# Two graph layers on one core: a second strip of A^T kept as bfloat16 for the last stage, its low bits checked during the sort

## The chip, the cores and the metric

The kernel runs on one core of one Trainium2 chip. The metric is the device time of one execution in microseconds (us). The engines are PE (matrix products; PEld is its weight load), DVE, ACT, POOL and SP; SP here only issues transfers, and POOL, ACT and SP each have transfer queues of their own. In the profile, q1 carries what SP issues here and q0 what POOL issues.

## The reference

Inputs: x (2708 x 128), a 0/1 matrix A (2708 x 2708), scalars alpha and beta, weights W (128 x 128) and a (1 x 256).

```python
# layer 0
adj_norm = dis[:, None] * adj * dis[None, :]          # dis = clip(degree, 1) ** -0.5
attn = softmax(beta * cosine(x) * adj, axis=1)
x = layernorm(x + adj_norm @ x - x + sigmoid(alpha) * (attn @ x - x))
# layer 1
XW = x @ W
s_col, s_row = XW @ a[0, :128], XW @ a[0, 128:]
den = exp(leaky_relu(s_row[:, None] + s_col[None, :]))
num = A @ den
att = where(num != 0, den / num, 0)
x = layernorm(x + A @ (att @ XW))
```

The matrix is 29 MB in float32. Nothing promises that its entries are 0 or 1: the kernel reads it as float32, and wherever it uses a bfloat16 form it proves while running that nothing was lost (below).

## The kernel before

Rows and columns are cut into 22 blocks of 128 (the last is partly filled) and into 6 strips of 512 columns (the last has 148, the "tail", from column 2560 on). The core holds only some of the matrix at a time, so it reads most of A^T (`adj_t`) several times. The stages, with their times in the profile:

1. Attention of layer 0, 0 to about 220 us.
2. Diffusion by strips of A^T, in the order 0, 5, 1, 2, 3, 4, to about 300 us. Strips 3, 4 and 5 stay in SBUF. While strips 0 and 5 are there, `low_bits_of` checks them (L175): ACT sums the absolute values of the lower 16 bits of each float32 word. If the sum is zero, the bfloat16 in the upper half is exactly the word.
3. The sort, about 295 to 357 us, overlapping the end of diffusion. Since leaky_relu has two slopes, rows are ordered by score and cut into 24 groups of at most 126. This stage computes scores, thresholds, one-hot tables and, from e^score, running row sums of A ("carries") into the PSUM tile `tot`. The sums need every column of A^T: strips 3 to 5 from SBUF (`kept_strips`, letter "k") and columns 0 to 1535 from HBM, row block by row block (`first_strips`, letter "e", L738). `fill("kke...")` strews these pieces between the other work. Each `first_strips` call lets SP load 128 x 1536 words (768 KB) into one of five rooms and PE do 12 small products `tot`. I count these loads in the order in which they are called and call them row 0 to row 21. Rooms: rows 0, 1, 2 and 7 share one room inside `x_sb`; the others take four rooms (`nat`) in turn, rows 3 to 6, then 8 to 11, 12 to 15, 16 to 19, and 20, 21 in the first two again. A load can start when all readers of the room's former row are done. Around these pieces the order of the stage is: the end of strip 2's layernorm and scores (`tr_sb`, `rstd`, `x`, `x_ps`, `sb_ps` into `sr_b`), the counting that gives the range of scores (`reach_b`), X@W in rows (`xw_ps`, copied by ACT into `att` and written to `xw_d`), thresholds (`thr_ps`, `k_gt`), one-hot tables (`k_hot`, `k_ons` and `j_ons` on ACT, `onp` on DVE, `tab_ps` on PE, copied by ACT into `k_t`, selected into `k_sel`), and last the carries copied out of `tot` and the table for the other index (`j_t`, `gb`), behind which the loop's first `num` waits.
4. The main loop over the 24 groups (357 to 585 us, about 8.83 us a step): an indirect gather on POOL fetches 126 rows of A^T into a ring of four, PE forms `num`, DVE and ACT divide, PE multiplies by gathered XW. In 11 of the steps POOL also issues a transfer that copies two blocks of strip 0 to HBM as bfloat16 (`a16_d`).
5. The last stage, 586 to 669 us: H = A @ M with M split into `m_hi` and `m_lo`. A^T streams in chunks through six rooms (the four of the ring, `wt`, `xws`); a chunk is rounded to the F32R type by DVE into one of three `rounded` tiles, its low bits are checked by ACT (the results of all checks select a general kernel at the end if anything was lost), and PE multiplies (`products`, L1612). `PARTS` are column ranges: 512 to 1536, 1536 to 2560 (22 float32 chunks of 1 MB, 2 blocks x 1024 columns each) and 0 to 512, read from `a16_d` (6 bfloat16 chunks, 4 blocks each, 0.5 MB) and widened by ACT or POOL. The tail's columns (`last`) come by one transfer on POOL's queue at the stage's start (L1552); their 44 products are written in the middle of the second part. `finished` (L1565) copies a part's sums, transposes them back and does residual, layernorm and output.

Order: in the attention's first strip and from the end of diffusion through the loop, "strict" mode pins every DVE, PE, POOL and ACT instruction issued through `dve`, `mm`, `gps`, `act` to the program's order on its engine. An engine in strict mode runs nothing out of turn: an instruction whose input is late holds all behind it. SP's loads are in order too. The last stage is not strict; there a scheduler interleaves.

Of the kernel before, what the change touches and what calls it, by code (L numbers as in the profile page):

```python
# [10 lines left out]
BF16 = mybir.dt.bfloat16  # L11
F32R = mybir.dt.float32r
I16 = mybir.dt.int16
AF = mybir.ActivationFunctionType
ALU = mybir.AluOpType
AX = mybir.AxisListType
# [2 lines left out]
P = 128  # L19
N = 2708  # L20
# [16 lines left out]
EARLY = 3  # L37
LAG = 2
TAIL = (NS - 1) * SW
PARTS = ((SW, 3 * SW), (3 * SW, TAIL), (0, SW))  # L40
RAISED = (1, 2, 3, 4)
KEPT = 3
LIMIT = 16.0
# [5 lines left out]
def grouped(  # L49
# [125 lines left out]
    def low_bits_of(a, room):  # L175

        low = a.bitcast(I16).rearrange("p (n t) -> p n t", t=2)[:, :, 0]
        i = len(seen)
        seen.append(i)
        nc.scalar.activation(  # L180
            room[:, : a.shape[1]], low, AF.Abs, accum_out=low_bits[:, i : i + 1]
        )

    cnt = const.tile([P, NS, 2, 2], F32, name="cnt")
# [498 lines left out]
    low = late.tile([P, NB], F32, name="low")  # L683
    e2_p = late.tile([P, NB], F32, name="e2_p")
    e2_w = late.tile([P, 3, NB, 2], BF16, name="e2_w")
    e2_r = late.tile([P, NB], F32, name="e2_r")
    ct = late.tile([P, 4], F32, name="ct")
    pinned("POOL", nc.gpsimd.memset, e2_w, 0.0)
# [46 lines left out]
    summed = [*range(12), 20, 21, *range(12, 20)]  # L735
    rooms = [0, 0, 0, 1, 2, 3, 4, 0] + [1, 2, 3, 4] * 4

    def first_strips(kb, eng):  # L738
        room = rooms[summed.index(kb)]
        if room == 0:  # L740
            a = x_sb.rearrange("p b d -> p (b d)")[:, : KEPT * SW]
        else:
            tag = (None, "x_hi0", "x_lo0", "x_hi1", "x_lo1")[room]
            a = nat.tile([P, KEPT * SW], F32, tag=tag, name="nat")
        eng.dma_start(a, adj_t[ts(kb, P), : KEPT * SW])
        for part in range(3):
            for q in range(4):
                sum_part(part, 0, q, kb, 0, a[:, ts(q, quarters[0])])
# [495 lines left out]
    valued("j", 1, j_hot, cs_p, 12)  # L1244
    fill("ee")
    assert not any(jobs.values()), jobs
    tmp.tile([P, P], F32, name="spare")
    j_own = chosen("j", j_hot, j_run, j_ahead)

# [202 lines left out]
    for step in range(NG + LAG):  # L1452
        g, before, first = step, step - 1, step - LAG
        if g < NG:
            qs[g] = flow.tile([P, N], F32, tag="q", name="q", bufs=LAG + 2)
        for s, item in enumerate(strips_m):
            if first == 0 and s < NS - 1:
                weigh(first, *item)
            if g < NG:
                multiply(g, *item)  # L1460
                if (g, s) == (0, 1):
                    j_no.append(numbers())
                    gather_xw(0)
                    gather(3)
                    gather_xw(1)
                if (g, s) == (0, 4):
                    weights(2, gb[:, 2, :])
                if item[2] == half or s == NS - 1:
                    carry(g, *parts_m[s // 3])
                    if g == 0:  # L1470
                        if s < 3:
                            weights(1, gb[:, 1, :])
                        log(0, *parts_m[s // 3])
            if 0 <= before < NG and s < 2:
                divide(before, *parts_m[s])
            if first > 0 and s < NS - 1:
                weigh(first, *item)
                if first == NG - 1:
                    to_mt(s)
                    if s > 1:  # L1480
                        m_rows(s - 2)
        if 0 <= before < NG:
            for i0, i1 in (parts_m[0], (half, TAIL), (TAIL, N)):
                power(before, i0, i1)
        if g < NG:
            if g > 0:
                for i0, i1 in parts_m:
                    log(g, i0, i1)
            if 3 <= g + 2 < NG:
                weights(g + 2, (gb[:, g + 2, :] if g < 2 else wt[:, g + 2, P - G :]))  # L1490
            if g + RING < NG:
                gather(g + RING)
            if g + 2 < NG:
                gather_xw(g + 2)
        if step == 1:
            spread_out_weights(8, NG)
        if 3 <= step < 3 + NB // 2:
            b0 = 2 * (step - 3)
            gps(
                "dma_start",  # L1500
                a16_d[:, b0 * SW : (b0 + 2) * SW].rearrange("p (b i) -> p b i", i=SW),
                adj_t[b0 * P : (b0 + 2) * P, :SW].rearrange("(b p) i -> p b i", p=P),
            )
        if step == NG:
            accs.append(ps_num.tile([P, SW], F32, tag="num", name="m_tail"))
            weigh_tails(range(first + 1))
# [98 lines left out]
    def banks_for(p0, p1):  # L1605
        hs = [(h, min(h + SW, p1 - p0)) for h in range(0, p1 - p0, SW)]
        return [ps_m.tile([P, SW], F32, tag="m", name="h_acc") for _ in hs], hs

    def products(kb, rows, hacc, hs):
        for part, m in enumerate((m_hi, m_lo)):  # L1610
            for acc, (h0, h1) in zip(hacc, hs):
                nc.tensor.matmul(  # L1612
                    acc[:, : h1 - h0], m[:, kb, :], rows[:, h0:h1],
                    start=(kb, part) == (0, 0), stop=(kb, part) == (NB - 1, 1),
                )

    short_by = [nc.scalar.copy, nc.gpsimd.tensor_copy, nc.scalar.copy] * 2
    short_by = short_by[::-1]
    for p0, p1 in PARTS:
        w_ = p1 - p0  # L1620
        hacc, hs = banks_for(p0, p1)
# [1 line left out]
        for kb in range(0, NB, step):  # L1623
            n = min(step, NB - kb)
            room = h_rooms[k % len(h_rooms)]
            k += 1
            if p0 == 0:
                a = room.bitcast(BF16)[:, : n * w_]
                nc.sync.dma_start(a, a16_d[:, kb * w_ : (kb + n) * w_])
                t = rounded(short_by.pop(), a)  # L1630
            else:
                a = room[:, : n * w_]
                nc.sync.dma_start(
                    a.rearrange("p (b i) -> p b i", b=n), rows_at(kb, n, p0, p1)
                )
                t = rounded(nc.vector.tensor_copy, a)
                low_bits_of(a, hp.tile([P, 2048], I16, tag="junk", name="junk", bufs=1))
            for b in range(n):
                products(kb + b, t[:, b * w_ : (b + 1) * w_], hacc, hs)
            if waiting and kb > 0:  # L1640
                waiting.pop(0)()
            if p0 == PARTS[1][0] and kb == NB // 2 + 1:
                last_banks = banks_for(TAIL, N)
                for b in range(NB):
                    products(b, last[:, b, :], *last_banks)
                waiting += finished(TAIL, NB - TAIL // P, *last_banks)
        if p0 == PARTS[-1][0]:
            while waiting:
                waiting.pop(0)()
# [5 lines left out]
            nc.tensor.matmul(no_ps[:, 0:1], ones, wild[:, 1:2], start=True, stop=True)  # L1655
            odd = late.tile([P, 1], mybir.dt.int32, name="odd")
            dve("tensor_scalar", odd, no_ps[:, 0:1], 0.5, None, ALU.is_gt)
        waiting += finished(p0, (w_ + P - 1) // P, hacc, hs)
    while waiting:
        waiting.pop(0)()  # L1660
    l1.close()
# [436 lines left out]
```

## Time and profile before

| | us |
|---|---|
| median of 3 runs | 672.46 (672.36 to 673.21) |
| profiled execution, whole | 670.93 |
| its span | 669.2 |
| PE busy in the span | 626.8 (94%) |
| DVE busy | 483.7 (72%) |
| ACT busy | 485.8 (73%) |
| POOL busy | 257.1 (38%) |
| bytes moved, mean rate | 179.90 MB, 269 GB/s |

The profile is of one execution. A "busy" share is an average over stages that have different limits, so stretches of the span are read one by one below. A row of a timeline is: start, duration, engine, line, operation, output <- inputs, sizes, count, and in brackets how long the engine stood idle before it and what it waited for. "SPq" and the like are the issue of a transfer, not its length.

### The profile page before, as it was taken

How to read it: one execution, taken by the hardware profiler on the slowest of the kernel's cores; microseconds unless marked ns; L12 is line 12 of the kernel's file. 1: busy time of each engine (PE TensorE's matmuls, PEld its weight loads, DVE VectorE, ACT ScalarE, POOL GpSimd, SP SyncE). 2: the span in 40 equal slices, each digit the busy share in tenths (PEclk: the TensorE clock that was granted, in tenths of full speed). 3: DMA queues.
4: the chain of work that ended last, by engine and by line, in shares of the span. 5: the costliest groups of instructions: out<-in, count | busy, mean ns of one | idle time of the engine just before them, and what ended most of it. 6: DMA issues, size and time to landing. Idle time of an engine off the chain costs nothing.

```text
span 669.2 us, 8587 instructions
## 1 busy us (share of the span) xinstructions
PE 626.8 (94%) x2859; PEld 355.1 (53%) x2859; DVE 483.7 (72%) x989; ACT 485.8 (73%) x671; POOL 257.1 (38%) x261
## 2 busy tenths in 40 slices
PE   7999999999999999999768899999999999996994
PEld 4445453545547477666544344444444444674873
DVE  5776876747655465848684999999999998497435
ACT  4767777868875653321474999999999999598761
POOL 5976788787985311100122233333322220010021
PEclk9999999999997999999987899999999999999798
DMA  8958989998999999989877998666655553399951
GB/s 269 349 195 277 361 309 338 352 329 297 311 287 389 331 387 384 386 266 355 320 293 187 240 232 230 189 191 183 183 185 205 169 189 106 112 308 387 414 204 51
DMA packets 68710, 179.90 MB, mean 269 GB/s; under 512 B 6986, under 2 KB 21716, under 8 KB 65636
## 3 DMA queue, kind: packets, MB, share of 16 engines
q1 hardware_dynamic: 45044, 114.45, 48.9%
q0 software_dynamic: 22224, 63.08, 32.3%
q10 hardware_dynamic: 1392, 1.77, 0.8%
q8 instruction: 24, 0.39, 0.2%
q14 instruction: 26, 0.21, 0.1%
HBM read 179.33 MB, written 5.72 MB: 277 GB/s over the span
## 4 chain that ended last, share of the span: by engine, by line
PE 60%; DMA 16%; issue 8%; DVE 7%; ACT 6%; POOL 2%; another core or an unknown queue 0%; DVEq 0%; SPq 0%; ACTq 0%; POOLq 0%
PE num L195 14%; PE m_acc L195 12%; PE att_acc L204 10%; PE sim L204 8%; DMA strip<-in_adj_t 6%; PE h_acc L1612 5%; DMA last<-in_adj_t 5%; DMA row<-in_adj 3%; PE dif_acc L204 3%; ACT row L195 1%; PE dif_acc L195 1%; PE tot L195 1%; PE sim L195 1%; POOL ss L195 1%; ACT xn L195 1%
## 5 line engine op out<-in xcount | busy, mean ns | idle before, releaser
L220 POOL TENSOR_TENSOR total<-total,p_t 128x512 f32<-128x512 f32 (+3 forms) x111 | 125.3, 1130 | 33.6 <-ACT p_t L214 27.9
L195 PE MATMUL m_acc<-q,xws 128*128 128x512 f32 x240 | 122.5, 596 | 0.0
L209 DVE SCALAR_TENSOR_TENSOR p_t<-sim,gentle,piece 128x512 f32<-128x512 f32 (+1 forms) x111 | 72.2, 671 | 47.3 <-PE sim L204 37.5
L195 PE MATMUL num<-ring,wt 128*128 128x512 f32 x216 | 98.4, 548 | 2.7 <-DVE q L195 2.0
L204 PE MATMUL att_acc<-p_t,x_sb 128*128 128x512 f32 (+1 forms) x228 | 96.5, 549 | 2.1 <-ACT p_t L214 1.9
L214 ACT ACTIVATE p_t<-p_t,shift 128x512 f32<-128x512 f32 (+1 forms) x111 | 69.4, 655 | 36.8 <-DVE p_t L209 31.7
L195 DVE COPY q<-num 128x512 f32<-128x512 f32 (+1 forms) x142 | 85.7, 615 | 13.6 <-PE num L195 13.6
L195 DVE SCALAR_TENSOR_TENSOR q<-sr_b,nc_s,q 128x1536 f32<-128x1536 f32 (+1 forms) x48 | 77.8, 1623 | 6.5 <-ACT q L195 6.0
L195 PEld LDWEIGHTS m_acc<-q,xws 128*128 128x128 f32 x240 | 45.5, 191 | 55.6 <-issue 55.3
L195 ACT ACTIVATE q<-q,head,rest 128x1536 f32<-128x1536 f32 (+1 forms) x48 | 70.2, 1508 | 2.8 <-DVE ring L195 2.5
L195 ACT ACT_TABLE_LOAD x52 | 66.7, 1283 | 3.6 <-issue 2.7
L195 PEld LDWEIGHTS num<-ring,wt 128*128 128x128 f32 x216 | 39.2, 191 | 48.0 <-issue 35.1
L204 PEld LDWEIGHTS att_acc<-p_t,x_sb 128*128 128x128 f32 x228 | 40.1, 197 | 44.7 <-ACT p_t L214 23.5
L195 ACT ACTIVATE q<-q,c_s 128x1536 f32<-128x1536 f32 (+1 forms) x48 | 63.0, 1355 | 0.3
L195 ACT ACTIVATE row<-row 128x1354 f32<-128x1354 f32 x44 | 58.1, 1321 | 4.4 <-DMA row<-in_adj 4.3
L195 POOL DMA_INDIRECT ring<-in_adj_t,k_no x18 | 21.0, 1169 | 89.3 <-PE num L195 88.4
L204 PE MATMUL sim<-xn_t 128*128 128x512 f32 (+1 forms) x102 | 47.4, 581 | 0.0
L1612 PE MATMUL h_acc<-rounded,m_hi 128*128 128x512 f32 x110 | 38.9, 418 | 2.0 <-DVE rounded L1557 1.8
L1612 PE MATMUL h_acc<-rounded,m_lo 128*128 128x512 f32 x110 | 37.4, 405 | 0.0
L195 PE MATMUL num<-x_sb,wt 128*128 128x512 f32 (+1 forms) x72 | 35.4, 585 | 0.7 <-ACT gb L195 0.7
L195 POOL DMA_INDIRECT xws<-xw_d,j_no x24 | 28.3, 1180 | 18.5 <-DVE c_s L195 11.5
L195 DVE COPY ring<-q 2x1536 f32<-2x1536 f32 (+1 forms) x36 | 30.8, 855 | 2.7 <-ACT q L195 1.4
(334 smaller groups left out, 1047.5 us busy)
## 6 DMA issues: line engine op xcount, KB each, us to landing
row<-in_adj SPq DMA_DIRECT2D x44, 677.0 KB, 5.6
piece<-in_adj_t SPq DMA_DIRECT2D x24, 1024.0 KB, 6.9
strip<-in_adj_t POOLq DMA_DIRECT2D x6, 2816.0 KB, 17.5
nat<-in_adj_t SPq DMA_DIRECT2D x18, 768.0 KB, 6.3
ring<-in_adj_t SPq DMA_DIRECT2D x12, 1024.0 KB, 9.2
strip<-in_adj_t SPq DMA_DIRECT2D x2, 2816.0 KB, 14.4
strip<-in_adj_t POOLq DMA_DIRECT2D x2, 2048.0 KB, 13.6
x_sb<-in_adj_t SPq DMA_DIRECT2D x4, 1024.0 KB, 7.3
```

Source lines behind the costliest of these rows:

```text
L195: latest[engine] = op(*args, **kwargs)
L204: op(*args, **kwargs)
L209: return getattr(nc.vector, op)(*args, **kwargs)
L214: return getattr(nc.scalar, op)(*args, **kwargs)
L220: getattr(nc.gpsimd, op)(*args, **kwargs)
L1612: nc.tensor.matmul(acc[:, : h1 - h0], m[:, kb, :], rows[:, h0:h1], start=(kb, part) == (0, 0), stop=(kb, part) == (NB - 1, 1),)
```

## The change

Columns 512 to 1023 ("strip 1") join columns 0 to 511 as bfloat16. In the loop the copying transfers go from 11 of two blocks to 12 of four (two of the twelve have two), still one a step, steps 3 to 14. In the last stage strip 1 is read from the copy: the float32 part is now 1024 to 2560 in a part of width 1024 and a part of width 512, and twelve bfloat16 chunks follow, widened by POOL and ACT in turn. The tail's products are written behind the float32 parts rather than in the middle of the second.

As strip 1 is no longer read as float32 there, its low bits are checked elsewhere: on the rows of the sort. Each `first_strips` call begins by having ACT check columns 512 to 1023 of the row loaded by the call before (`low_bits_of_row`, 22 in all, the last one after the last sum). `low_bits_of` now goes through `act`, so the checks hold their place in ACT's strict order.

```diff
-PARTS = ((SW, 3 * SW), (3 * SW, TAIL), (0, SW))
+SHORT = 2 * SW
+PARTS = ((SHORT, 4 * SW), (4 * SW, TAIL), (SW, SHORT), (0, SW))
@@ low_bits_of
-        nc.scalar.activation(
-            room[:, : a.shape[1]], low, AF.Abs, accum_out=low_bits[:, i : i + 1]
+        act(
+            "activation", room[:, : a.shape[1]], low, AF.Abs,
+            accum_out=low_bits[:, i : i + 1],
         )
@@ the sort
+    low_row = late.tile([P, SW], I16, name="low_row")
+    unseen = []
+    def low_bits_of_row():
+        low_bits_of(unseen.pop()[:, SW:SHORT], low_row)
     def first_strips(kb, eng):
+        if unseen:
+            low_bits_of_row()
         room = rooms[summed.index(kb)]
...
         eng.dma_start(a, adj_t[ts(kb, P), : KEPT * SW])
+        unseen.append(a)
...
     assert not any(jobs.values()), jobs
+    low_bits_of_row()
@@ the loop
-        if 3 <= step < 3 + NB // 2:
-            b0 = 2 * (step - 3)
+        if 3 <= step < 3 + 12:
+            s, b0 = divmod(4 * (step - 3), 24)
+            n = min(4, NB - b0)
             gps(
                 "dma_start",
-                a16_d[:, b0 * SW : (b0 + 2) * SW].rearrange("p (b i) -> p b i", i=SW),
-                adj_t[b0 * P : (b0 + 2) * P, :SW].rearrange("(b p) i -> p b i", p=P),
+                a16_d[:, s, b0 : b0 + n, :],
+                adj_t[b0 * P : (b0 + n) * P, ts(s, SW)].rearrange(
+                    "(b p) i -> p b i", p=P
+                ),
             )
@@ the last stage
-    short_by = [nc.scalar.copy, nc.gpsimd.tensor_copy, nc.scalar.copy] * 2
-    short_by = short_by[::-1]
+    short_by = [nc.scalar.copy, nc.gpsimd.tensor_copy] * 6
...
-            if p0 == 0:
+            if p0 < SHORT:
                 a = room.bitcast(BF16)[:, : n * w_]
-                nc.sync.dma_start(a, a16_d[:, kb * w_ : (kb + n) * w_])
+                nc.sync.dma_start(a, a16_d[:, p0 // SW, kb : kb + n, :])
...
-            if p0 == PARTS[1][0] and kb == NB // 2 + 1:
-                last_banks = banks_for(TAIL, N)
-                for b in range(NB):
-                    products(b, last[:, b, :], *last_banks)
-                waiting += finished(TAIL, NB - TAIL // P, *last_banks)
...
-        waiting += finished(p0, (w_ + P - 1) // P, hacc, hs)
+        waiting += finished(p0, w_ // P, hacc, hs)
+        if p0 == PARTS[1][0]:
+            last_banks = banks_for(TAIL, N)
+            for b in range(NB):
+                products(b, last[:, b, :], *last_banks)
+            waiting += finished(TAIL, NB - TAIL // P, *last_banks)
```

More of the change, by code (lines that the diff above doesn't have):

```diff
@@ L13 @@
 I16 = mybir.dt.int16
+U16 = mybir.dt.uint16
 AF = mybir.ActivationFunctionType
@@ L2086 @@
     ]
-    a16_d = nc.dram_tensor("a16_d", (P, NB * SW), BF16, kind="Internal").ap()
+    a16_d = nc.dram_tensor("a16_d", (P, 2, NB, SW), BF16, kind="Internal").ap()
     xw_d = nc.dram_tensor("xw_d", (NP, D), F32, kind="Internal").ap()
```

## The prediction

> **What bounds the kernel now.** I read the table of windows first, to see which stage is bound by what; then ACT's and SP's timelines through the sort, since the change adds work to ACT there and SP's loads hang on it; then the chain of waits, and PE's timeline and the transfers in the last stage.
>
> The sort, in windows of 10 us: columns are length, then busy us (count) of PE, PEld, DVE, ACT, POOL, then PE's clock, the DMA share and GB/s.
>
> ```profile
> 290.00:300.00 10.00, 9.55 (x47) 6.17 (x46) 3.60 (x10) 0.36 (x1) 0.00 (x0) 1.00 0.69 240
> 300.00:310.00 10.00, 8.12 (x168) 5.18 (x172) 7.27 (x31) 1.50 (x4) 0.00 (x0) 1.00 0.98 371
> 310.00:320.00 10.00, 10.00 (x168) 8.76 (x161) 9.27 (x53) 2.77 (x6) 0.00 (x0) 1.00 0.74 264
> ```
>
> ACT is nearly empty here (0.36, 1.50, 2.77 of 10). By share alone the new checks are free. But ACT is in strict order, and its timeline shows what the idle time waits for:
>
> ```profile
> 299.64 0.58 ACT L195 COPY tr_sb<-dif_acc 128x512 f32<-128x512 f32 x1 [10.88 <-PE dif_acc L195]
> 303.74 0.30 ACT L195 ACTIVATE rstd<-mv,eps 128x4 f32<-128x4 f32 x1 [3.01 <-DVE mv L195]
> ...
> 322.27 0.37 ACT L195 COPY att<-xw_ps 128x256 f32<-128x256 f32 x1 [0.32 <-PE xw_ps L195]
> ...
> 348.57 0.27 ACT L195 COPY k_t<-tab_ps 128x128 f32<-128x128 f32 x1 [1.69 <-remote]
> ```
>
> SP issues row 2's load as soon as row 1's sums are done (PE's `tot` of row 1: 295.97 to 296.57), and PE consumes it at 301.26 with no wait:
>
> ```profile
> 296.62 0.33 SPq L745 DMA_DIRECT2D x_sb<-in_adj_t  x1
> ```
>
> ```profile
> 301.26 0.69 PE L195 MATMUL tot<-x_sb,e_w 128*2 128x384 bf16 x12
> ```
>
> The chain of waits shows that one later load is already late in the stage; a row takes 4.1 to 9.4 us from issue to landing (median 6.3; in the `x_sb` room 4.1 to 7.0, median 5.5):
>
> ```profile
> 322.89 5.53 DMA nat<-in_adj_t
> ```
>
> The last stage: the transfers are full (1.03 to 1.18) from 590 to 640, and PE stands once, for the tail:
>
> ```profile
> 619.78 0.49 PE L1612 MATMUL h_acc<-last,m_hi 128*128 128x148 f32 x1 [5.70 <-DMA last<-in_adj_t]
> ```
>
> From there to the last product at 659.0 PE stands little more. Why `last` takes 33.73 us (586.01 to 619.74), though it has only 1.67 MB, the queues say (here from 594 to 600):
>
> ```profile
> q1 hardware_dynamic: 522, 2.01, 89.1%
> q0 software_dynamic: 524, 0.31, 24.6%
> ```
>
> As many packets of `last` (592 bytes) go as packets of SP's queue (4 KB): one for one. So `last` gets 592/(592+4096) = 13% of the bytes.
>
> **The last stage.** Float32 chunks go from 22 MB to 16.5, bfloat16 from 2.88 MB to 5.77: 2.6 to 2.9 MB less, at the measured 385 to 417 GB/s 7 us of transfer. PE's work is the same (220 products of 512 columns, 44 of 148), so what counts is when PE waits. Chunks of the second float32 part now have rows of 2 KB, not 4. That is chunk 11 on; before, it was rounded at 610.13, one pace of 3.05 us after it began, about 607. Until then `last` goes as before, 50 GB/s x 21 us = 1.05 MB; then its share is 592/(592+2048) = 22%, 87 GB/s (estimate from those packets), and the other 0.62 MB take 7.1 us: it lands at 614.1, not 619.74. In both kernels PE has the first tail products behind chunk 11 (its order on the engine says so), which before ended at 613.8.
> Onward: chunk 12 lands at 614, then one every 2.55 us (the pace before, without `last`), each rounded in 1.22 and multiplied in 1.88. Chunk 15 and the half chunk 16 end at 625.9, the other 23 tail products (0.11 each) at 628.4, 88 products of bfloat16 parts (0.235 each, from 2.81 us for 12) at 649.1, the transposes (1.5) at 650.6. Take 651 against 659.0: 8.0 gained. In it are the 5.7 of standing and the 2.6 that the following products took too long: the clock is 0.70 in 620 to 630, and eight products took 3.5 us, not 1.88. Casts: 12, alternating ACT (1.89 to 1.92) and POOL (1.91), one chunk per 1.88 of PE, so two engines hide them. The five fewer DVE roundings and ACT checks of 128x2048 here are hidden either way. Bounds: 1.2 if `last` lands as before (only the stands of 0.25 and 0.79 at 643 and 646 go), 9.3 at most (stands and cold stretch all gone).
>
> A page speaks against this gain. The Trainium skill's "DMA: Bandwidth & Descriptors" (SWDGE vs HWDGE vs iDMA) says an engine switches between queues at packet boundaries, with packets of preferably up to 4096 bytes and many descriptors. By it, halving a row leaves the shares as they are and the gain at 1.2, which would make the sum 687.0. The one-for-one row above decides for me.
>
> **The loop.** The copying transfers move 0.52 MB more read and 0.26 more written per step. The trace shows a share of 0.60 to 0.73 in 440 to 510, and POOL issues such a copy in 0.75 us, then stands 5.65 us for PE's `num` before the next gather. A gather has three steps (26 us) of lead. I cost it at nothing; cover gone, one issue per step: 12 x 0.75 = 9 us.
>
> **The sort.** A check of 128x512: the 2048-wide one has a pitch of 2.03 us with its accumulator read (597.51, 599.54), a 1536-wide one runs 1.48 against 1.91, so 0.83 ns per column: 2.03 - 1536 x 0.00083 = 0.75 us. 22 of them are 16.5 us of ACT, which idles more than that. What costs is their place. A row's room is free only after ACT's check, which has ACT's in-order waits ahead of it. Three places, in times of before:
>
> 1. Row 0's check stands behind `rstd` of 288.47, so row 1's load goes at 289.6 instead of 257.9 and lands around 295; its sums are due at 295.97: nothing. Row 1's check stands behind the next `rstd` (303.74 + 0.30), so row 2's load goes at 304.8, not 296.62, and lands 4.1 to 5.5 later, 308.9 to 310.3. PE, in order, stands from 301.3. Then 2.5 us of sums that stood ahead of `x_ps` (301.26 to 303.8), `x_ps` 1.0, DVE's copy 0.68, so `sb_ps` at 313.0 at the earliest against 306.89. After standing that long PE is slow: 42 table products took 2.56 us after 3.75 idle, 1.40 when warm. That adds up to 3. Delay 5.6 to 8.5; I take 7.5, nearer to the cold row.
> 2. Row 12's load waits for row 8's check, behind the last `att` copy (322.64), and row 13's for the next check: issued at 323.4 and 324.15, landing about 328.9 and 330.7. Sums of row 13 began at 328.45, thresholds at 329.13; they come 2.2 later (1.5 to 4).
> 3. Rows 18 to 20 wait for checks behind the table work; row 21's load waits for row 17's check behind the `k_t` copy of 348.57: 349.6 against 344.04, beside the loop's first three gathers (4.1 MB). At 6.3 it lands at 355.8, sums were due at 349.7. The carries' copies, in order behind it, wait: 6.0 (3 to 9).
>
> Together 15.7 (10 to 21.5). Rows 3 to 11 have slack: those loads were issued 5 to 10 us ahead of use. The loop cannot win it back, for the last carry stands ahead of its first `num` at 356.92.
>
> **Sum.** +15.7 - 8.0 + 0 = +7.7. The profiled execution took 670.93 (span 669.2), 1.53 under the median; it would become 678.6, the median 672.46 + 7.7 = **680.2 us**.
>
> **The rivals.**
> - Faster: the checks are hidden. If ACT's and SP's order leaves row loads their lead, only the gain stays: 672.46 - 8.0 = 664.5. For it: ACT's idle share. Against: row 2's load, 4.7 us ahead of use, against a check that cannot run before 304.04. It decides when row 2 lands before 301.3.
> - `last` lands no sooner (packets do not go one for one at 2 KB): gain 1.2, so 672.46 + 14.5 = 687.0. For it: PE's order still puts tail products behind chunk 11. Against: the packet counts.
> - Only the first place costs (later rows have enough lead): 7.5 - 8.0 = -0.5, 672.0. For it: the medians of landing hide a best case of 4.1. Against: 322.89 5.53, a late load already on the chain.
> - The loop's copies are on the path: +9, 689. For it: PE, DVE and ACT are all full there. Against: POOL's 5.65 of idle and the gather's lead.
>
> **How the numbers follow.** Main case 0.58, its own range 676 to 685 (bounds of the three places, not all at one end); checks hidden 0.10; `last` no sooner 0.14; first place only 0.07; loop 0.11. A measurement can tell about 0.2%, 1.3 us, from no change. Faster: 0.10 and 0.02 of the middle case, 0.12. Same: 0.03. Slower: 0.85. The range 674 to 688 leaves out the 0.10, most of the 0.07 and half of the loop case: 0.2.
>
> **What would show it.** In the changed profile: row 2's load at about 305 and a stand of PE of some 8 us for DMA `x_sb` before 310; a clock under 1.00 there; the loop's first `num` at 372 rather than 356.92, and 228 us for the loop as before; `last` landing in some 28 us rather than 33.73; last products 8 us sooner after the loop's end than the 73 of before. I am wrong if row 2's load goes early, if the loop's steps grow beyond 8.83, or if PE still stands over 4 us for `last`.

## The result, and the profile after

The changed kernel takes **692.02 us** (median of 4 runs, 690.61 to 693.43) against 672.84 us for the kernel before, measured beside it (672.36 to 677.64). The ratio is 1.027, with a 95% interval from 1.0215 to 1.0322. It is slower, as forecast, but by 19.2 us and not by 7.7, and above the range of 674 to 688.

The profiled execution has a span of 689.0 us (before: 669.2). I cut both spans at the same three events: the first transposition `tr_ps` in the strict order of the sort (284.87 before, 285.43 after), the loop's first `num`, and the issue of the transfer of `last`.

| us | to the sort's first `tr_ps` | the sort, to the first `num` | the loop, to the issue of `last` | last stage |
|---|---|---|---|---|
| before | 284.87 | 72.05 | 229.09 | 83.19 |
| after | 285.43 | 100.14 | 226.03 | 77.40 |
| difference | +0.56 | **+28.09** | -3.06 | -5.79 |

The stage table of each experiment below is cut in the same way. The first column moves between executions by several us (284.9 to 295.6), and of the edits of this study only two work there (the checks left to the scheduler, and the check in the diffusion); so whole times are compared as medians, and stages by these cuts.

The sort is where the time went, in three stands of PE. The views follow in the order in which I read them. First the windows of after (columns: length, then busy us and count of PE, PEld, DVE, ACT, POOL, then PE's clock, the DMA share and GB/s):

```profile
290.00:300.00 10.00, 9.93 (x48) 6.52 (x48) 4.16 (x12) 0.00 (x0) 0.00 (x0) 1.00 0.69 238
300.00:310.00 10.00, 1.81 (x31) 1.02 (x34) 4.72 (x25) 2.49 (x6) 0.00 (x0) 0.67 0.69 236
310.00:320.00 10.00, 9.72 (x191) 6.03 (x183) 4.20 (x16) 4.32 (x13) 0.00 (x0) 0.82 0.72 244
360.00:370.00 10.00, 2.44 (x26) 1.14 (x26) 2.74 (x2) 5.28 (x19) 2.48 (x2) 0.57 1.03 275
370.00:380.00 10.00, 1.87 (x32) 1.26 (x35) 0.77 (x4) 1.56 (x6) 0.00 (x0) 0.50 0.91 219
```

PE is busy 1.81 us in 300 to 310, where it was busy 8.12 before, and its granted clock falls to 0.67 there; from 360 to 380 it does 4.3 us of work in 20 at a clock of 0.50 to 0.57. ACT is busy at most 5.28 us of 10 in these windows. It is nearly full only from 350 to 360 (9.27, with the one-hot tables; before, 8.35 in 330 to 340). So most of the loss is not ACT's time; what the loads wait for is the checks' place in its order.

PE's timeline of after says what it stood for (in brackets):

```profile
309.46 1.13 PE L198 MATMUL tot<-x_sb,e_w 128*2 128x384 bf16 x12 [7.46 <-DMA x_sb<-in_adj_t]
...
337.39 1.03 PE L198 MATMUL tot<-nat,e_w 128*2 128x384 bf16 x12 [3.92 <-DMA nat<-in_adj_t]
...
378.13 1.13 PE L198 MATMUL tot<-nat,e_w 128*2 128x384 bf16 x12 [10.68 <-DMA nat<-in_adj_t]
...
641.17 0.34 PE L1629 MATMUL h_acc<-last,m_hi 128*128 128x148 f32 x1 [1.05 <-DMA last<-in_adj_t]
```

The first three rows are the three places of the prediction. PE stands there for rows 2, 12 and 21 of the sort: at the second place it is row 12, whose load went at 331.68 (below), that is late; row 13 follows at 340.33 without a wait. The last line is the stand for the tail, 5.70 before and 1.05 now. PE also stood 4.05 us for row 20 at 366.32, but row 21's load had gone before that and landed later, so it alone sets the end. Before, the sums of rows 20 and 21 ran without a wait:

```profile
349.22 1.19 PE L195 MATMUL tot<-nat,e_w 128*2 128x384 bf16 x24
```

ACT's timeline shows the check that stands ahead of each of those three loads:

```profile
304.30 0.30 ACT L198 ACTIVATE rstd<-mv,eps 128x4 f32<-128x4 f32 x1 [3.01 <-DVE mv L198]
304.50 0.61 ACT L198 ACTIVATE low_row<-x_sb 128x512 int16<-128x512 int16 x1
...
330.66 0.37 ACT L198 COPY att<-xw_ps 128x256 f32<-128x256 f32 x1 [0.32 <-PE xw_ps L198]
330.93 0.63 ACT L198 ACTIVATE low_row<-nat 128x512 int16<-128x512 int16 x1
...
360.64 0.27 ACT L198 COPY k_t<-tab_ps 128x128 f32<-128x128 f32 x1 [0.97 <-remote]
360.80 0.63 ACT L198 ACTIVATE low_row<-nat 128x512 int16<-128x512 int16 x1
```

Each check stands directly behind an instruction that waited for other work: `rstd`, the last copy into `att`, and the `k_t` copy. The chain of waits of after (start, length, what) then has each load at the end of its check:

```profile
304.50 0.71 ACT low_row L198 x2
305.23 4.19 DMA x_sb<-in_adj_t
...
331.68 5.67 DMA nat<-in_adj_t
...
361.55 16.54 DMA nat<-in_adj_t
```

The last line is the surprise: row 21's load took 16.54 us. The transfers from 361 to 378 say what it shared the queues with (queue, packets, MB, share of 16 engines):

```profile
q0 software_dynamic: 389, 3.25, 78.7%
q1 hardware_dynamic: 173, 0.88, 21.9%
```

Queue q0 is POOL's, and these are the first three gathers of the loop, issued ahead of the load, as POOL's timeline shows:

```profile
356.95 1.18 POOL L198 DMA_INDIRECT x_sb<-in_adj_t,k_no  x1 [24.67 <-DVE k_no L198]
358.43 1.06 POOL L198 DMA_INDIRECT ring<-in_adj_t,k_no  x1 [0.30 <-PE tab_ps L198]
359.80 2.48 POOL L198 DMA_INDIRECT ring<-in_adj_t,k_no  x1 [0.30 <-issue]
```

The queues did not take turns from the start. From 361.5 to 367 SP's queue moved 20 packets (0.10 MB) and POOL's 134 (1.36 MB); from 367 to 370 it was 54 against 53.

In the last stage the two queues still go one packet for one, now with packets of 2 KB on SP's side (transfers from 630 to 636):

```profile
q1 hardware_dynamic: 780, 1.69, 83.2%
q0 software_dynamic: 778, 0.46, 36.5%
```

### The profile page after: what moved, and what is told of

Same layout as the page of the kernel before. It is cut to its first block, busy times and chain, and to the rows that moved or that the text cites. A ratio compares the mean times of both kernels' runs of the same rounds, so it can differ in the third digit from the quotient of the medians.

```text
span 689.0 us, 8642 instructions
## 1 busy us (share of the span) xinstructions
PE 626.9 (91%) x2859; PEld 355.3 (52%) x2859; DVE 480.1 (70%) x984; ACT 493.8 (72%) x707; POOL 267.8 (39%) x266
## 4 chain that ended last, share of the span: by engine, by line
PE 72%; DMA 10%; DVE 7%; ACT 5%; issue 3%; POOL 1%; another core or an unknown queue 0%; DVEq 0%; SPq 0%; ACTq 0%; POOLq 0%
PE num L198 15%; PE m_acc L198 15%; PE att_acc L207 12%; PE sim L207 9%; PE dif_acc L207 5%; PE h_acc L1629 4%; DMA nat<-in_adj_t 3%; DMA strip<-in_adj_t 3%; DMA x_sb<-in_adj_t 3%; PE tot L198 2%; PE dif_acc L198 1%; PE tab_ps L198 1%; PE sb_ps L207 1%; PE sim L198 1%; POOL ss L198 1%
## 5 line engine op out<-in xcount | busy, mean ns | idle before, releaser
L217 ACT ACTIVATE p_t<-p_t,shift 128x512 f32<-128x512 f32 (+1 forms) x111 | 69.3, 655 | 33.3 <-DVE p_t L212 28.1
L198 DVE SCALAR_TENSOR_TENSOR q<-sr_b,nc_s,q 128x1536 f32<-128x1536 f32 (+1 forms) x48 | 77.8, 1623 | 5.6 <-ACT q L198 5.1
L1629 PE MATMUL h_acc<-rounded,m_hi 128*128 128x512 f32 x110 | 41.5, 408 | 2.6 <-DVE rounded L1574 1.7
L1629 PE MATMUL h_acc<-rounded,m_lo 128*128 128x512 f32 x110 | 40.0, 396 | 0.0
L198 PEld LDWEIGHTS <-e_w 128*2 128x2 bf16 x648 | 16.6, 90 | 36.2 <-issue 33.9
L198 PE MATMUL tot<-nat,e_w 128*2 128x384 bf16 x216 | 14.4, 387 | 20.9 <-DMA nat<-in_adj_t 20.9
```

The lines of the kernel that those rows point to most:

```text
L198: latest[engine] = op(*args, **kwargs)
L217: return getattr(nc.scalar, op)(*args, **kwargs)
L1629: nc.tensor.matmul(acc[:, : h1 - h0], m[:, kb, :], rows[:, h0:h1], start=(kb, part) == (0, 0), stop=(kb, part) == (NB - 1, 1),)
```

## The experiments

The theory, P: ACT's row checks cost all of the loss, by their place; the bfloat16 part alone gains what the last stage shows. The first rival, D: something else of the change, such as the larger copies in the loop, costs too. The second, L: the 3 us by which the loop is shorter are a gain of the change. Further questions come up on the way: what made row 21's load so long, and whether the check can be had for nothing somewhere else.

**The change without its row checks.** Twice, in two sessions.

```diff
     def first_strips(kb, eng):
-        if unseen:
-            low_bits_of_row()
         room = rooms[summed.index(kb)]
...
     assert not any(jobs.values()), jobs
-    low_bits_of_row()
```

> The changed kernel without the checks of strip 1 on the rows of the sort (the proof that strip 1's bfloat16 copy loses nothing is left out; all else stays). In the changed profile the first num stands 28.7 us later than before, and from there to the end it is 8.9 us shorter: about 3.1 up to the start of the last stage, 5.8 in the last stage. Theory P (the checks' place in ACT's order makes the row loads late): all of the 28 goes, the 5.8 of the last stage stay, and the 3.1, which I put down to gathers that had time to land during the delay, go too: 667 us, ratio 0.991. Rival L (the loop's 3.1 is a real gain of the change): 664. Rival D (something else of the change delays the sort): above 672.

Measured: 665.54 us, ratio 0.988 (0.981 to 0.995). The sort takes 73.24 us, the loop 227.25, the last stage 76.90. PE's windows of this kernel show the sort as it was before:

```profile
290.00:300.00 10.00, 9.02 (x41) 6.82 (x41) 5.47 (x30) 3.66 (x5) 0.00 (x0) 1.00 0.76 202
300.00:310.00 10.00, 9.09 (x124) 5.54 (x122) 5.36 (x20) 1.31 (x3) 0.00 (x0) 1.00 0.90 338
```

So the rest of the change gains 7 to 8 us, and all of the loss hangs on the checks. The time lies between the 667 of P and the 664 of L and does not separate them. The kernel with the checks alone (below) does: its loop has no larger copies and takes 225.55 us, so a short loop is no gain of the change.

> The changed kernel without the row checks once more (the proof for strip 1 left out), beside the kernel of this call that has them all, so that both stand against the same runs of before: by the first run 0.988 of before (0.981 to 0.995); by the stages of the profiles the last stage gains 6.3 and the sort loses 0 to 1, so 0.990 to 0.992. If the kernel with all checks comes within 0.002 of it, the checks are hidden.

Measured: 666.23 us, ratio 0.989 (0.984 to 0.993); stages 71.71, 225.53, 76.93. It repeats.

**The row checks alone, in the kernel before.** The kernel before with `low_bits_of` through `act` and the 22 row checks; loop and last stage untouched.

```diff
+    low_row = late.tile([P, SW], I16, name="low_row")
+    unseen = []
+    def low_bits_of_row():
+        low_bits_of(unseen.pop()[:, SW : 2 * SW], low_row)
     def first_strips(kb, eng):
+        if unseen:
+            low_bits_of_row()
...
         eng.dma_start(a, adj_t[ts(kb, P), : KEPT * SW])
+        unseen.append(a)
...
     assert not any(jobs.values()), jobs
+    low_bits_of_row()
```

> The kernel before with only the row checks of the change, in ACT's strict order; parts, copies and the last stage as before. Theory P: the whole delay of 28 us less the 3 of the loop's start, no gain at the end: 672.8 + 25 = 698 us. Rival D (other parts of the change, such as the larger copies, contribute to the delay): below 692.

Measured: 698.15 us, ratio 1.037 (1.030 to 1.044): 25 us for the checks by themselves. The sort takes 98.75, the last stage 83.06 as before. PE's timeline of this kernel has all three stands again (the second, 3.37 us, at 338.86), and row 21's load takes 16.28 us:

```profile
311.68 0.81 PE L196 MATMUL tot<-x_sb,e_w 128*2 128x384 bf16 x8 [7.35 <-DMA x_sb<-in_adj_t]
...
378.23 1.13 PE L196 MATMUL tot<-nat,e_w 128*2 128x384 bf16 x12 [10.82 <-DMA nat<-in_adj_t]
```

The two halves add up: +25.4 and -7.2 (672.74 to 665.54, same session) give +18.2; the whole change measured +19.2. Theory P stands.

**Is the order on ACT the cause, or ACT's reading of the room?** The checks stay, but are not pinned to the strict order.

```diff
-        act(
-            "activation", room[:, : a.shape[1]], low, AF.Abs,
-            accum_out=low_bits[:, i : i + 1],
-        )
+        nc.scalar.activation(
+            room[:, : a.shape[1]], low, AF.Abs, accum_out=low_bits[:, i : i + 1]
+        )
```

> The changed kernel with one word of the change undone: the checks go to ACT directly, not through the strict order, so that the scheduler places them. The same 22 checks, the same 16.5 us of ACT, but the first two now stand before the sort and row 17's ahead of the k_t copy. Theory P (place): the row loads go early, the delay of 28 us falls to under 4, 667 to 671 us. Rival W (the work of the checks on ACT costs, wherever it stands): the delay stays above 16 us, 683 or more.

Measured: 679.66 us, ratio 1.011 (1.007 to 1.015), between the two expectations. The sort's delay falls from 28.1 to 7.8 us (79.84 against 72.05), so 20.3 us of it hang on the strict order. But the scheduler put the checks of rows 0 and 1 into ACT's work in the diffusion, where ACT stood for the row:

```profile
254.21 0.63 ACT L182 ACTIVATE low_row<-x_sb 128x512 int16<-128x512 int16 x1 [4.82 <-DMA x_sb<-in_adj_t]
```

ACT stood 4.82 and 5.64 us for rows 0 and 1, and that stretch of the diffusion grew from 49.9 to 54.1 us (from the first `tr_sb` copied out of `dif_acc` to the sort's first `tr_ps`). Of the two, row 1's load and its check are on the chain of waits. The same stretch took 52.0 and 49.7 us in the two kernels without row checks, so the growth is 2 to 4 us. The order moves a part of the loss about: a check that stands early makes what is behind it wait for the row.

**What made row 21's load long?** Two kernels: row 17's check pinned earlier, and two of the three gathers issued later.

```diff
+    low_bits_of_row()
     valued("k", 1, k_hot, low, 17)
```

> The changed kernel with one check moved: row 17's goes ahead of the work of the second table, so row 21's load need not wait for the k_t copy at 360.64 and can be issued at about 356.5 instead of 361.56, ahead of most of the three gathers' traffic (issued 356.95 to 359.80). Theory P with the gathers as the price of the third place: it lands in 6 to 10 us, at 363 to 367 instead of 378, and 9 to 13 us go, less up to 3 that the loop's start then waits for gathers: 680 to 685 us. Rival G (any load beside the three gathers ends only with them, about 376 to 378): no gain over 2 us, 689 to 692.

Measured: 686.42 us, ratio 1.021 (1.012 to 1.029); 1.4 us outside the first expectation and below the rival's. The edit moved row 21's load as far as was meant: it was issued at 360.00, which is 5.5 us earlier from the stage's start than in the changed kernel, and 1.0 us ahead of the first gather (361.01). But it took 13.94 us and not 6 to 10. The loads of rows 18 to 20 had gone only 1.6 to 3.6 us before it, and from 368 to 374 SP's queue moved just 7 packets (0.03 MB) while the gathers moved 1.33 MB. In the second kernel without row checks the same load has nearly the same lead (348.54 against 349.36), but the load before it had gone 8 us earlier, and it is there after 4.3 us. The sort takes 91.99 us, 8.2 less.

```profile
373.98 1.13 PE L198 MATMUL tot<-nat,e_w 128*2 128x384 bf16 x12 [7.67 <-DMA nat<-in_adj_t]
```

```diff
-    def gather(g):
+    def gather(g, idx=None):
+        idx = k_no if idx is None else idx
...
-    gather(1)
-    gather(2)
+    k_late = tab.tile([P, NG], mybir.dt.uint32, name="k_late")
+    dve("tensor_copy", k_late[:G], k_no[:G])
+    gather(1, k_late)
+    gather(2, k_late)
```

> The changed kernel with one wait added: the second and third gather of the loop take their row numbers from a copy that DVE makes behind the check of row 21, so row 21's load has only the first gather (1.37 MB) beside it, not three (4.1 MB). If the 16.54 us of that load are the price of the gathers: it lands in 6 to 10 us, the last sums come 7 to 10 us sooner, and since the two gathers then land later, 1 to 4 us come back at the loop's start: 683 to 688 us. If the load is slow for another cause (its queue, its room, the late rows 18 to 20 ahead of it): it still takes 14 us or more and the time stays at 690 or goes above.

Measured: 687.33 us, ratio 1.017 (1.012 to 1.022), as expected. With one gather beside it (issued at 362.59; the other two at 377.95 and 379.32), row 21's load took 10.14 us and PE stood 5.74 rather than 10.68:

```profile
375.65 1.13 PE L198 MATMUL tot<-nat,e_w 128*2 128x384 bf16 x12 [5.74 <-DMA nat<-in_adj_t]
```

So two of the three gathers are some 6 of the 16.5 us, by a run that moved them and left the load nearly where it was (74.5 us after the stage's start, against 76.1). The sort takes 93.17, 7.0 less. The expected price of the late gathers did not come: the loop takes 225.55 us. The median falls by 4.7, by 6.4 if each kernel is set against the kernel before that ran beside it.

**The check at the row's own place.** Each row is checked right behind its own sums instead of at the next call, so the check of a row stands a call earlier in ACT's order.

```diff
     def first_strips(kb, eng):
-        if unseen:
+        if kb == 1:
             low_bits_of_row()
...
+        if kb > 0:
+            low_bits_of_row()
-    low_bits_of_row()
```

> The changed kernel with the same 22 checks on ACT in strict order, but each at the place of its own row's sums, not at the call of the next row (row 0's stays ahead of row 1's load). So row 1's check stands ahead of tr_sb and rstd, row 9's directly behind the att copies, row 17's between the two tables, and rows 18 to 21 free no room that is needed. Theory P (place alone): all three delays go, the sort is at most 3 us longer than without checks, the last stage's 6 us stay: 665.5 (without checks) to 669 us, ratio to before 0.988 to 0.995. Rival W (work on ACT costs: 16.5 us of checks, of which the run with the scheduler's places still lost 7.8 in the sort): 672 or more.

Measured: 673.57 us, ratio 0.998 (0.995 to 1.001). That is outside P's range and in that of the rival W. The sort takes 77.80 us: of the delay of 28.1, 5.7 stay. PE stands 3.56 us for row 13:

```profile
332.61 0.68 PE L198 MATMUL tot<-nat,e_w 128*2 128x384 bf16 x12 [3.56 <-DMA nat<-in_adj_t]
```

That is not where the rest comes from: the thresholds (`thr_ps`) come 46.1 us after the stage's start, against 44.1 to 46.0 in the kernels whose sort has no row checks, and PE stands 1.6 to 1.8 for that row there too. But from the thresholds to the first `num` it is 31.7 us, against 27.3 to 29.1. In that stretch the checks of rows 20 and 21 stand on ACT between the last sums, which end at 356.7, and the copy of the carries (PE's timeline, then ACT's):

```profile
354.57 2.09 PE L198 MATMUL tot<-nat,e_w 128*2 128x384 bf16 x24
```

```profile
357.74 0.61 ACT L198 ACTIVATE low_row<-nat 128x512 int16<-128x512 int16 x1
...
358.48 0.63 ACT L198 ACTIVATE low_row<-nat 128x512 int16<-128x512 int16 x1
...
359.24 0.93 ACT L198 COPY x_sb<-tot 2x384 f32<-2x384 f32 x2
```

The chain of waits from 340 to 365 has 3.0 us of checks in it. So a few us are ACT's time after all, as W has it, and about 20 are the place: the same 22 checks, the same ACT time, one call earlier, and 18.5 us less in the medians (20.2 against the kernel before beside each). It is the most direct evidence that the place is what costs most.

**Are the 5.7 us that stay ACT's time?** The same kernel, but rows 18 to 21 are checked by DVE behind the one-hot tables (maximum of the absolute values of the lower halves).

```diff
+        if kb > 0 and len(seen) < 26:
+            low_bits_of_row()
...
     j_onp = placed("j", j_own, (0, 12, NB))
+    for a in unseen:
...
+        dve("tensor_reduce", low_bits[:, i : i + 1], low_row, AX.X, ALU.max,
+            apply_absolute_value=True)
```

> The kernel with each check at its own row's place, with one more move: the checks of rows 18 to 21 leave ACT, where they stood in front of j_ons, kt and the carries' copies (4 x 0.74 us), and DVE makes them in its idle 4 us behind onp. In the run with all 22 on ACT the sort took 77.8 us from the last tr_ps of strip 3 to the first num, against 72.1 to 73.5 in the four kernels whose sort has no checks. Theory P with the checks' own time on ACT's path at the end: 2 to 4 of these 5 us go, 74 to 76 us, and the time comes to 0.990 to 0.996 of before. Rival (the 5 us are row loads that still come late, or the noise of transfers): no change, 0.998.

Measured: 673.46 us, ratio 1.000 (0.997 to 1.003): a miss. The sort takes 79.37 us; PE stands 3.38 us for row 21, 3.41 for row 13 and 1.23 for row 2, all for their loads (of row 13 the kernels without row checks have 1.6 to 1.8 too):

```profile
363.82 1.13 PE L198 MATMUL tot<-nat,e_w 128*2 128x384 bf16 x12 [3.38 <-DMA nat<-in_adj_t]
```

The checks are off the path now: ACT copies the carries at 365.00, directly behind the last sums (364.95). But row 21's load, which took 8.31 us here and 4.3 without row checks, is on the chain in their place. So the run does not clear ACT's time. It exchanges one wait for another, and no run took both away; how the remaining 5 to 7 us divide between late loads and ACT's time stays open.

**The loop's larger copies alone.** The kernel before, with the twelve copies of four blocks in its loop; the last stage reads only strip 0 of them, as before.

```diff
-        if 3 <= step < 3 + NB // 2:
-            b0 = 2 * (step - 3)
+        if 3 <= step < 3 + 12:
+            s, b0 = divmod(4 * (step - 3), 24)
+            n = min(4, NB - b0)
...
```

> The kernel before with only the loop's larger copies: both strips are copied to bfloat16, the second is not used. If the copies are hidden (the forecast's zero): 672.7, ratio 0.998 to 1.002, and the loop from first num to the tail's issue stays at 229 us. If each of the twelve issues is on the path: 681.5.

Measured: 673.85 us, ratio 0.998 (0.995 to 1.001). The loop takes 225.53 us: the copies are hidden, and the rival in which they are on the path is out.

**The narrow float32 parts alone.** The kernel before, with its wide parts cut in two; no bfloat16 strip more, and as many bytes as before.

```diff
-PARTS = ((SW, 3 * SW), (3 * SW, TAIL), (0, SW))
+PARTS = ((SW, 2 * SW), (2 * SW, 3 * SW), (3 * SW, TAIL), (0, SW))
...
-            if p0 == PARTS[1][0] and kb == NB // 2 + 1:
+            if p0 == PARTS[2][0] and kb == 0:
```

> The kernel before with one thing changed: its first float32 part of 1024 columns is cut into two parts of 512, so the chunks ahead of and beside the tail's transfer have rows of 2 KB instead of 4 from the start of the last stage. Bytes, copies and checks as before. If queues take turns packet by packet, the tail's share rises from 13% to 22% from the start and it lands 19 to 23 us after its issue instead of 33.7; PE's stand of 5.7 us for it goes; 664 to 670 us. If its pace goes by bytes or its own queue: 33 to 34 us, the stand stays, 671 to 674 us.

Measured: 672.5 us, ratio 0.998 (0.994 to 1.001). `last` landed as expected: issued at 589.50, and its queue is empty from about 612.6 on, so some 23 us against 33.73. The transfers from 599 to 604 and from 612 to 615 of this kernel:

```profile
q1 hardware_dynamic: 688, 1.36, 82.2%
q0 software_dynamic: 690, 0.41, 38.8%
```

```profile
q1 hardware_dynamic: 419, 1.21, 101.8%
q0 software_dynamic: 65, 0.03, 5.3%
```

But the time that I expected from it (664 to 670) did not come; 672.5 is what the other case gave, though not by its way. The last stage is only 1.6 us shorter (81.60). PE no longer stands once for the tail; it waits chunk by chunk (5.4 us in six stands for rounded chunks, 1.8 in the kernel before), and the chain of waits of that stage is now the chunks' transfers:

```profile
by line: PE m_acc L195 13.4%; PE num L195 13.0%; PE att_acc L204 12.3%; PE sim L204 9.2%; DMA wt<-in_adj_t 6.2%; issue 5.8%; PE dif_acc L204 5.1%; DMA strip<-in_adj_t 3.2%; DMA wt<-g_d 3.0%; PE h_acc L1612 1.6%; DMA x_sb<-in_adj_t,k_no 1.3%
```

Here `wt<-in_adj_t` (chunks of A^T in the last stage) has 6.2% of the whole span, 41 us in three transfers, half of the last stage. `h_acc`, the products, has 13% of that stage, while in the kernel before it and `last` had 41% each. An earlier tail alone gained nothing clear of noise; with fewer bytes as well it gains the 6 us of the last stage.

**The check on the loop's gathered rows, by POOL.** The gathers fetch every row of A^T anyway, and POOL stands there; so POOL adds up the lower halves of each gathered tile, and ACT checks the sum once.

```diff
+            raw = ring[g % RING][:, SW:SHORT].bitcast(U16)
...
+            gps("tensor_copy", lows, raw.rearrange("p (n t) -> p n t", t=2)[:, :, 0])
+            gps("tensor_tensor", bits, bits, lows, ALU.add)
             if g + RING < NG:
                 gather(g + RING)
...
+    act("activation", bits, bits, AF.Abs, scale=rest, accum_out=low_bits[:, i : i + 1])
```

> The changed kernel with the check of strip 1 moved out of the sort: every row of A^T also passes through the loop's ring, raw, 126 rows a step. Ahead of each gather POOL, which stands 5.6 us there, widens the lower halves of columns 512 to 1023 of the ring tile in use to float32 and adds them to a running sum (two instructions of 128x512, about 1.1 us each by POOL's rows of that size); at the end ACT checks the sum once, with the two carry rows masked. The sort is that of before. Theory P (the checks cost by the rooms that they hold and by ACT's order in the sort): sort 72 to 73.5 us, loop 225 to 229, last stage 77: 665 to 668 us, ratio 0.987 to 0.992, as without checks. Rival C (24 x 2.3 us of POOL in the loop delay the gathers, or slow DVE, which is over 90% busy there): the loop grows by 3 us or more, 669 and up.

Measured: 678.1 us, ratio 1.004 (1.001 to 1.008): the rival, 13 to 15 us more in the loop. The sort is undisturbed (74.08), but the loop takes 240.31 us (227.25 and 225.53 without row checks). POOL has room (54.1 us busy of 80 from 420 to 500), and yet DVE's steps got longer. The groups of this kernel, and then of the change without row checks (columns behind the bar: busy us, mean ns of one, idle before):

```profile
L198 DVE SCALAR_TENSOR_TENSOR q<-sr_b,nc_s,q 128x1172 f32<-128x1172 f32 x24 | 44.0, 1834 | 0.0
```

```profile
L198 DVE SCALAR_TENSOR_TENSOR q<-sr_b,nc_s,q 128x1172 f32<-128x1172 f32 x24 | 34.3, 1430 | 0.0
```

Two of POOL's instructions and the DVE instruction beside each show how (the timelines of POOL, then of DVE, in the POOL-checked kernel):

```profile
430.10 2.53 POOL L198 TENSOR_TENSOR bits<-bits,lows 128x512 f32<-128x512 f32 x1
...
439.31 1.28 POOL L198 TENSOR_TENSOR bits<-bits,lows 128x512 f32<-128x512 f32 x1
```

```profile
430.06 1.43 DVE L198 SCALAR_TENSOR_TENSOR q<-sr_b,nc_s,q 128x1172 f32<-128x1172 f32 x1
...
439.28 2.54 DVE L198 SCALAR_TENSOR_TENSOR q<-sr_b,nc_s,q 128x1172 f32<-128x1172 f32 x1
```

At 430 DVE has its normal 1.43 and POOL's addition takes 2.53; at 439 POOL has its 1.28 and DVE takes 2.54. Each time one of the two has its own length and the other about the sum of both. The Trainium skill's "SBUF — State Buffer" (Who interferes with whom) states that DVE and GpSimd share a pair of ports as an exclusive lock, also for a DVE instruction with two SBUF inputs against a GpSimd instruction that reads SBUF, and that whoever comes first holds it for the whole instruction. These rows agree that one of the two waits for the whole of the other. Who came first they do not show: at 439 DVE's recorded start is 0.03 us the earlier, and DVE is the one that took 2.54. All instructions of this kind together, of both widths, grew from 77.8 to 91.9 us in the loop, as much as the loop itself; that they are its whole loss is argued from this sum, and no run isolates it.

**The check where the strip lies in SBUF anyway.** During the diffusion strip 1 is in SBUF, as strips 0 and 5 are when they are checked; here it is checked there, in six pieces, instead of on the rows of the sort.

```diff
-        if s in (0, NS - 1):
+        if s in (0, 1, NS - 1):
             flat = strips[s].rearrange("p b i -> p (b i)")
-            cuts = (0, 4, 8, 11, 15, 19, NB) if s == 0 else (0, NB // 2, NB)
+            cuts = (0, 4, 8, 11, 15, 19, NB) if s < 2 else (0, NB // 2, NB)
```

> The changed kernel with strip 1 checked neither in the sort nor in the loop but in six pieces in the diffusion, while the strip lies in SBUF, as strips 0 and 5 are (there the words are as the F32R load left them, so the proof holds only if that load keeps all bits; otherwise nothing is left out). Six checks of 1.7 to 2.1 us on ACT, which in the profile of before stands about 10 of the 13 us from 242 to 255; strip 3's load into the same room waits for the last of them. Theory P: the sort is as before, the diffusion from its first tr_sb to the last tr_ps of strip 3 grows from 50 to at most 54 us, the last stage keeps its 6 us: 666 to 670 us, ratio 0.989 to 0.996. Rival (any place of 11 us of checks ahead of the loop costs about what it takes): 676 or more.

Measured: 667.27 us against 670.88 beside it, ratio 0.992 (0.988 to 0.995), as expected: 0.8% under the kernel before, with an interval clear of 1, and a good part of the 1.1 to 1.2% that the change without checks gains. Its profiled execution (673.97 us) has the sort at 71.35, the last stage at 77.16, and the stretch of the diffusion at 53.4. One reservation: strips 0 and 5 lie in tiles of float32, while strip 1 is transferred into a tile of the F32R type. The check proves something about the words in HBM only if that transfer keeps their lower bits, and no run here tried that. The kernel copies the chunks of the last stage into the same type to round them, so until it is tried this run measures the place and is not a kernel to use.

## Why the prediction was right in direction and wrong in size

**Row 2's load (7.5 predicted).** Right, in its way and in its size. The load was issued at 305.23 (predicted 304.8), landed 4.19 us later, PE stood 7.46, and `sb_ps` came at 315.26 against 306.89: 8.4, of which 0.56 is the shift of the stage's start, so 7.8. The clock was 0.67 in that window; the table products' cold price, from which the 7.5 was taken, fits.

**The second place, row 13's load (2.2 predicted, 1.5 to 4).** Right mechanism, at the upper end. The row that PE stood for is row 12, whose load the prediction named but whose sums it did not price; row 13 came behind it without a wait. Thresholds (`thr_ps`) at 341.24 against 329.06 are 12.2 late, 3.8 more than at `sb_ps`.

**Row 21's load (6.0 predicted, 3 to 9).** This is the step that failed. The first `num` came at 385.57 against 356.92, 28.65 late, so this place cost 16.5 us. The wait was the one named, the check behind the `k_t` copy, and the gathers beside it were named too. What failed is the term "At 6.3 it lands at 355.8": the median of loads in an emptier stretch was used for a load that has 4.1 MB of gathers ahead of it. It took 16.54 us. An upper end could have been worked out from rows at hand: the load's 0.79 MB and the gathers' 4.1 at the 264 GB/s of the kernel before in 310 to 320 are 18.5 us. With that for the 6.3 the sum goes up by 12 to about 692. The runs on this load bear out that the gathers are what it met: 16.28 us again in the kernel with the checks alone, 13.94 when it was issued just ahead of them with other loads still under way, 10.14 with one gather beside it, 4.3 when it went ahead of them alone.

**The loop (0 predicted).** Right: the larger copies alone left its length as it was. The 3 us by which the loop of after is shorter than that of before are no gain of the change: but for the kernel with POOL's check, the loops of all kernels here take 225.5 to 229.7 us, with the larger copies and without.

**The last stage (8.0 predicted).** Direction right, 5.8 measured (6.3 without the row checks). `last` landed 29.5 us after its issue, against 28.1 predicted. The stand of 5.70 fell to 1.05 and PE's busy time in the stage from 65.4 to 63.1, because the cold stretch (a clock of 0.66 in 616 to 626) is gone; that is the 2.6 of the prediction, 2.3 measured. What is missing to 8.0 is small: `last` came 1.4 us later than predicted, so 1.05 of the stand stays; PE waits 0.73 for a widened chunk at 669.7, which the prediction took as hidden; and from the last product to the end it takes 0.4 longer. PE's waits for rounded chunks are as before (1.7 us after 1.8), so the 0.25 and 0.79 that were to go came back at other chunks. That PE runs into the pace of the chunks once it does not stand for `last` shows in the kernel with narrow parts alone.

The Trainium skill's "DMA: Bandwidth & Descriptors" (SWDGE vs HWDGE vs iDMA), as the prediction read it, would have put this gain at 1.2 (the two stands named for that bound, 0.25 and 0.79, make 1.04). The measurement decides against that reading. In the rows of after, 780 packets went against 778 at 2 KB, and 688 against 690 in the kernel with narrow parts alone: one for one, as the rows before had it at 4 KB; and with narrow parts alone, at the same bytes, `last` landed after some 23 us and not 33.73.

**The sum.** Predicted +15.7 - 8.0 + 0 = +7.7. Measured in the spans: +0.56 + 28.1 - 3.1 - 5.8 = +19.8; in the medians +19.2. Of the 12 us between forecast and result, 10.5 are row 21's load alone, 1.9 the other two places, 2.2 the last stage and 0.6 the stage's start, less the 3 us of the loop, which no edit explains.

**The rivals.** "The checks are hidden" is out by the checks alone (+25.4). "Only the first place costs" is out by the rows 12 and 21. "The loop's copies are on the path" is out by the copies alone. "`last` lands no sooner" is out by its 29.5 us.

## What to carry to other kernels

An engine in strict order that becomes one more reader of a rotating room can delay the room's next load by its wait, however idle it is: ask for each such instruction what it stands behind and which load waits for it. 22 checks with 16.5 us of work, on an engine that is busy 43 of the 100 us from 290 to 390, cost 25 us, and the same checks one call earlier about 6 in the sort. A load that is pushed later must be priced by what is in the queues at its new time, in bytes over the rate of such a stretch, and not by its usual latency. And before a check is placed on a stream, look for a stage in which the data lies still anyway.

## What the runs showed of the hardware that was not expected

A load of 768 KB took 4.19 us in a quiet stretch, 16.54 us behind three gathers (4.1 MB), which had 3.25 of the 4.13 MB moved in that time. I had thought that the one-for-one turns of the queues would give the load its share; for its first 5.5 us it had 20 packets of 154. Nor did the queues here move gathers as fast as loads: in the kernel with row 17 checked early SP's queue moved 2.21 MB of loads from 360 to 366 (busy share 93%), POOL's 1.33 MB of gathers from 368 to 374 (102%).

DVE's `scalar_tensor_tensor` with two inputs from SBUF and POOL's `tensor_tensor` kept each other out in turn (1.43 to 2.54 us, 1.28 to 2.53), and the loop with this pair in each step took 13 to 15 us longer although POOL had idle time.
